# A two-layer decoder on one core: the mixer's product within sequences in two row halves, and the routed tokens in full and half tiles

## The chip, the core and the metric

The kernel runs on one core of a Trainium2 chip, in float32 throughout. The metric is the time of one execution in device microseconds. TensorE (PE) multiplies matrices, and its weight loads are shown as an engine of their own (PEld); VectorE is DVE, ScalarE is ACT, GpSimd is POOL, and SyncE (SP) issues transfers.

## What is computed

The input is 64 sequences of 64 tokens of width 256, so 4096 tokens. Two layers follow each other, each with three blocks that are added to the residual stream:

```python
x = x + mixer0(layernorm(x))        # Mamba-2 scan: 4 heads of 128, state 128, one chunk of 64 = one sequence
x = x + xattn0(layernorm(x), ctx)   # attention to ctx_512, 16 heads
x = x + moe0(layernorm(x))          # 7 routed experts, the best 2 of each token, and a shared one
x = x + wkv1(layernorm(x))
x = x + gqa1(layernorm(x), ctx)
x = x + ffn1(layernorm(x))          # 8 groups of experts, computed densely
```

The change touches the first and the third of them. In the mixer a sequence is one chunk, so what matters is the product within the chunk:

```python
L = exp(where(causal, log_diff, -inf))
CB = einsum('bcign,bcjgn->bcijg', C_c, B_c)
y_intra = einsum('bcijGH,bcijG,bcjGH,bcjGHp->bciGHp', L_rs, CB, dt_rs, x_rs)
```

The routed experts are

```python
_, ids = top_k(gate + gate_bias, 2)
u = xt @ Wup[e] + bup[e]
g = silu(u @ Wgate[e] + bgate[e]) * u
eo = g @ Wdown[e] + bdown[e]
out = sum over the two chosen experts of probs * eo, plus the shared expert
```

## The kernel before

**Order of the work.** `Net.run` (line numbers are those of the kernel before) runs three phases: `layer0` (mixer, attention, and for seven of the eight blocks of 512 tokens the front of the experts), `moe_phase` (the last front, the tables, the routed tiles, some of the shared expert), and `layer1`. Each phase is a set of generators ("streams") that are played by `Plan.play`: the planner keeps a time for each engine, prices every instruction with `Plan.cost` while the program is built, and always continues the stream that can begin first. A `yield` waits for what the stream has issued; `yield [1]` also asks for one free PSUM bank, `[2]` for two; a pair such as `("made", 3)` waits for a mark. The result is a fixed order of instructions on each engine. Every engine then works through its own list in that order, and all instructions carry the line of the helper that issues them (L60), so the profile tells them apart by the names of their tiles.

**The mixer.** `ssm_front` prepares half a block (256 tokens) and `ssm_tile` works on 128 tokens, that is two sequences; there are 32 such tiles. `ssm_tile` makes `cbm` (CB with the causal mask, on DVE), `ml` (the decays, an exponential on ACT), and then their product on POOL into `ssm_m`. `ssm_m` is one of two tiles that `w_ssm` zeroes once: 128 rows, 4 heads, 128 columns, in which sequence j fills the rows and the columns of its own 64 tokens and the rest stays zero. So two POOL instructions of 64 partitions write one tile. `xdt` (inputs times dt, transposed to tokens by rows) is the other factor. The product `py` is four matmuls, one for each head, of 128 rows by 128 columns into one PSUM bank; DVE multiplies all of it by the gate `sf_sg` into `y`, POOL adds `sf_g2`, and `po` is the output projection, which DVE adds to `x_sb`.

**The routed experts.** `moe_front` finds the two best experts of each token, and `moe_row` scatters its row (the normed token and its weight) to a slot of `moe_hs` in DRAM, where expert e owns the rows from 4096 e. `moe_tables` then counts on DVE: `n` is the number of tiles of 256 rows that each expert needs, `end` their running sum, `tab` (as integers `mt_int`) gives for each of the `MAXT` tiles its expert and its first row, and `left` the row of `moe_ys` in which each token's result will lie. MAXT is (8192 + 7 x 255) / 256 = 38, the most that seven experts can need. `moe_tile` loads for tile j the expert and row with `value_load` on SP, then by transfers the rows (`ht`), the expert's three matrices (`pack`) and a bias; it transposes the rows (`ht_ps`, `htT`), and `expert` computes u (`u_ps`, `uT`), g (`g_ps`, `gT`, with a DVE product) and d (`d_ps`). DVE adds the bias, ACT scales by the weight, and POOL issues the store to `moe_ys`. Six tiles may be loaded ahead, three be in work. The shared expert (`shared`, tiles `sh_hT`, `sh_w`) fills the time until the first routed tile begins; what is left of it goes to `layer1`, where `collect` gathers the routed results into `x_sb`.

In the routed phase TensorE's order for one tile is: transposes of the next tile, d of the tile before, g of this tile, u of the next.

Of the kernel before, what the change touches and what calls it, by code (L numbers as in the profile page):

```python
# [5 lines left out]
F32 = mybir.dt.float32  # L6
I32 = mybir.dt.int32
AF = mybir.ActivationFunctionType
# [4 lines left out]
P = 128  # L13
# [18 lines left out]
ET_PER_E = NBLK * TB // ET  # L32
MAXT = (2 * NBLK * TB + 7 * (ET - 1)) // ET
# [204 lines left out]
class Net:  # L238
# [86 lines left out]
    def w_ssm(self, side):  # L325
# [8 lines left out]

        w["m"] = []
        for i in range(2):
            t = wp.tile([P, 4, P], F32, name=f"ssm_m{i}")
            nc.gpsimd.memset(t, 0.0)
            w["m"].append(t)
# [156 lines left out]
    def ssm_tile(self, wk, w, n, t, f):  # L496
# [23 lines left out]
        m = w["m"][t]  # L520
        for r in seqs:
            gp.tensor_mul(m[r, :, r], ml[r], bc(cbm[r], 1, 4))
# [8 lines left out]
        yield self.after(("g2", n, 0), ("g2", n, 2), 1)  # L531
        py = self.mm([P, 4, P], "py")
        for q in range(4):
            te.matmul(py[:, q], xdt[:, q], m[:, q], start=True, stop=True)
        yield
        y = wk.tile([P, 4, P], F32, tag="y", bufs=2, name="y")
        v.tensor_mul(y, py, f["sg"][:, :, tok])
        self.give(py)
# [206 lines left out]

    def w_moe(self, side):
# [14 lines left out]
        w["thr"] = wp.tile([P, ET_PER_E], F32, name="moe_thr")  # L761
# [143 lines left out]
    def moe_tables(self, wk, w):  # L905
# [8 lines left out]
        gt, n, end = t("gt", [P, 7, ET_PER_E]), t("n", [P, 7]), t("end", [P, 7])  # L914
        v.tensor_tensor(gt, bc(cnt, 2, ET_PER_E), bc(w["thr"], 1, 7), ALU.is_gt)
        self.give(cnt)
        v.tensor_reduce(n, gt, AX.X, ALU.add)
        v.tensor_tensor_scan(end, w["ones"][:, 0:7], n, 0.0, ALU.mult, ALU.add)
        past, st, tab = t("past", [1, MAXT, 7]), t("st", [1, MAXT]), t("tab", [1, 2, MAXT])
        v.tensor_tensor(past, bc(end[0:1], 1, MAXT), bc(w["num"], 2, 7), ALU.is_le)  # L920
        v.tensor_reduce(tab[:, 0], past, AX.X, ALU.add)
        v.tensor_mul(past, past, bc(n[0:1], 1, MAXT))
        v.tensor_reduce(st, past, AX.X, ALU.add)
        v.tensor_sub(st, w["num"], st)
        v.tensor_scalar(st, st, float(ET), None, ALU.mult)
        v.scalar_tensor_tensor(tab[:, 1], tab[:, 0], float(SLOTS), st, ALU.mult, ALU.add)
        w["tab"] = wk.tile([1, 2, MAXT], I32, tag="mt_int", bufs=1, name="mt_int")
        v.tensor_copy(w["tab"], tab)

        off, of, left = t("off", [P, 7]), t("of", [P, NBLK * 2 * NT, 7]), t("left", [P, NBLK * 2 * NT])  # L930
        v.tensor_sub(off, end, n)
        v.scalar_tensor_tensor(off, off, float(ET), w["slot"], ALU.mult, ALU.subtract)
        v.tensor_mul(of, w["oh"].rearrange("p b k t e -> p (b k t) e"), bc(off, 1, NBLK * 2 * NT))
        v.tensor_reduce(left, of, AX.X, ALU.add)
        v.tensor_add(left, left, w["at"].rearrange("p b k t -> p (b k t)"))
        v.tensor_copy(self.left.rearrange("p b k t -> p (b k t)"), left)
# [4 lines left out]
    def moe_tile(self, wk, w, j):  # L941
        nc, te, v = self.nc, self.nc.tensor, self.nc.vector
        yield self.after(("tables", 0), ("tile", j - 6))
        e = nc.sync.value_load(w["tab"][0:1, 0, j:j + 1], min_val=0, max_val=7)
        r = nc.sync.value_load(w["tab"][0:1, 1, j:j + 1], min_val=0, max_val=ROWS - ET)
        h = wk.tile([P, 2, HW], F32, tag="ht", bufs=6, name="ht")
        rd = nc.sync.dma_start(h, w["hs"][bass.ds(r, ET)].rearrange("(i p) d -> p i d", p=P)).ins
# [7 lines left out]
        yield self.after(("made", j - 3), 1)  # L955
        ps = self.mm([P, 2, ET], "ht_ps")
        for c in range(2):
            for i in range(2):
                te.transpose(ps[:, c, i * P:(i + 1) * P], h[:, i, c * P:(c + 1) * P], self.ident)
        yield  # L960
        self.plan.mark("begun", j)
        hT = wk.tile([P, 2, ET], F32, tag="htT", bufs=3, name="htT")
        v.tensor_copy(hT, ps)
        self.give(ps)
        yield [1]
        ps = yield from self.expert(wk, m, hT, 3, False)
        y = wk.tile([P, 2, D], F32, tag="y", bufs=3, name="y")
        v.tensor_add(y, ps, bc(b, 1, 2))
        self.give(ps)
        yield  # L970
        for i in range(2):
            nc.scalar.activation(y[:, i], y[:, i], AF.Copy, scale=h[:, i, D:D + 1])
# [765 lines left out]
```

## Time and profile before

| what | us |
|---|---|
| median of 3 runs | 2133.9 |
| lowest and highest of them | 2132.7 and 2133.91 |
| the profiled execution's own time | 2130.03 |
| span of its trace, first to last instruction | 2128.3 |
| PE, DVE, ACT, POOL busy | 1943.1, 1343.9, 797.0, 871.3 |
| mean granted TensorE clock | 0.962 |

In a timeline a line gives the start and the length in us, the engine, the line of the kernel, the operation, the tiles it writes and reads, the shapes, how many records were merged (x8), and in brackets how long the engine had been idle before and what ended that. A matmul in float32 leaves two records, a transpose one. Matmuls overlap at their ends, so that the distance from the first start of a group to the first start of the next tells what the group costs. Shapes of a matmul are weights (rows*columns), then what is moved (rows x columns).

### The profile page before, as it was taken

The page shows a single profiled execution, that of the slowest core. Times are in us where ns is not written, and L with a number is a line of the kernel's source. Part 1 is how long each engine was busy: PE and PEld are TensorE (multiplying, and loading weights), DVE is VectorE, ACT ScalarE, POOL GpSimd, SP SyncE. Part 2 cuts the span into 40 slices and gives each one's busy share as a digit, 9 for nine tenths or more (in the row PEclk, how much of TensorE's full clock was granted, in tenths as well). Part 3 has the DMA queues.
Part 4 walks back from the last instruction along what each step waited for, and adds up shares of the span by engine and source line. Part 5 has one row for each costly group of instructions (what it writes and reads, how often), then busy time and mean ns, then how long its engine had stood idle before and what let it go on. Part 6 is the DMA issues. An engine that isn't in the chain of part 4 may idle for free. (4 is left out here: it accounts for less than half of the span.)

```text
span 2128.3 us, 35968 instructions
## 1 busy us (share of the span) xinstructions
PE 1943.1 (91%) x13515; PEld 1557.0 (73%) x13515; DVE 1343.9 (63%) x3080; ACT 797.0 (37%) x1445; POOL 871.3 (41%) x1079
## 2 busy tenths in 40 slices
PE   7998998989889997899997879979899999999998
PEld 6777787767667776788875647767677777777777
DVE  5668677777776764333336787887778676755331
ACT  3435343343434333344443433433334334343220
POOL 3333535345443423111126856666455344432211
PEclk9999999999989999999998879999999999999999
DMA  7965000001000011588844111121011101010010
GB/s 202 346 205 162 22 16 22 24 14 34 17 20 18 22 38 59 190 291 266 267 149 101 26 24 28 22 35 22 17 26 23 19 11 20 8 24 14 14 26 10
DMA packets 168765, 152.02 MB, mean 71 GB/s; under 512 B 76153, under 2 KB 156176, under 8 KB 168592
## 3 DMA queue, kind: packets, MB, share of 16 engines
q1 hardware_dynamic: 153232, 122.44, 19.8%
q0 software_dynamic: 15360, 27.28, 5.2%
q8 instruction: 107, 1.75, 0.3%
q14 instruction: 66, 0.54, 0.1%
HBM read 88.84 MB, written 60.83 MB: 70 GB/s over the span
## 5 line engine op out<-in xcount | busy, mean ns | idle before, releaser
L60 PE MATMUL gu_ps<-hT,ffn_gu 128*128 128x256 f32 x1408 | 337.6, 387 | 4.7 <-DVE gqa_q L60 3.9
L60 PEld LDWEIGHTS gu_ps<-hT,ffn_gu 128*128 128x128 f32 x1408 | 260.7, 192 | 50.4 <-issue 8.1
L60 PE MATMUL acc<-ffn_d,aT 128*128 128x256 f32 x704 | 165.5, 388 | 9.2 <-DVE aT L60 9.2
L60 POOL TENSOR_TENSOR aT<-aT,ffn_sc 128x512 f32<-128x512 f32 (+1 forms) x48 | 69.2, 1442 | 228.9 <-DVE aT L60 202.7
L60 PEld LDWEIGHTS acc<-ffn_d,aT 128*128 128x128 f32 x704 | 134.1, 194 | 34.2 <-DVE aT L60 10.7
L60 PE MATMUL proj<-sf_hT,w_in 128*128 128x256 f32 x640 | 152.3, 396 | 0.0
L60 ACT ACT_TABLE_LOAD x104 | 133.4, 1283 | 18.4 <-PE st L60 7.9
L60 PEld LDWEIGHTS proj<-sf_hT,w_in 128*128 128x128 f32 x640 | 124.5, 198 | 19.5 <-issue 1.6
L60 PE MATMUL po<-xa_vo,ctxT 128*128 128x256 f32 x512 | 119.0, 388 | 12.2 <-DVE ctxT L60 6.3
L60 ACT ACTIVATE aT<-gu_ps 128x512 f32<-128x512 f32 x96 | 48.7, 559 | 204.5 <-PE gu_ps L60 204.4
L60 DVE TENSOR_TENSOR aT<-aT,gu_ps 128x512 f32<-128x512 f32 x96 | 56.9, 633 | 106.2 <-ACT aT L60 106.2
L60 PE MATMUL q_ps<-xn_hT,xa_q 128*128 128x256 f32 x512 | 117.5, 385 | 4.4 <-ACT xn_hT L60 3.7
L60 PEld LDWEIGHTS po<-xa_vo,ctxT 128*128 128x128 f32 x512 | 97.5, 194 | 29.4 <-issue 11.3
L60 POOL DMA_INDIRECT x_sb<-moe_ys,left x64 | 106.3, 1661 | 20.4 <-issue 11.2
L60 POOL DMA_DIRECT2D moe_ys<-y x38 | 27.3, 717 | 212.8 <-ACT y L60 205.8
L60 PEld LDWEIGHTS q_ps<-xn_hT,xa_q 128*128 128x128 f32 x512 | 96.4, 192 | 23.5 <-ACT xn_hT L60 5.5
L60 POOL TENSOR_TENSOR ssm_m<-ml,cbm 64x256 f32<-64x256 f32 x64 | 46.4, 725 | 144.1 <-ACT ml L60 123.2
L60 DVE TENSOR_REDUCE gqa_q<-sc 128x8 f32<-128x512 f32 x128 | 79.2, 680 | 36.8 <-PE sc L60 34.1
L60 DVE SCALAR_TENSOR_TENSOR sf_acc<-proj,ssm_vec,sf_acc 128x252 f32<-128x252 f32 (+2 forms) x192 | 87.3, 472 | 11.3 <-ACT sf_acc L60 6.7
L60 POOL DMA_INDIRECT moe_hs<-moe_h,moe_slots x64 | 64.5, 1007 | 63.6 <-DVE moe_h L60 31.0
L60 DVE TENSOR_TENSOR x_sb<-x_sb,po 128x256 f32<-128x256 f32 x64 | 26.4, 413 | 98.3 <-PE po L60 98.2
L60 POOL TENSOR_TENSOR p<-p,sm 128x1024 f32<-128x1024 f32 x32 | 60.6, 1901 | 56.0 <-DVE sm L60 39.7
(338 smaller groups left out, 4381.9 us busy)
## 6 DMA issues: line engine op xcount, KB each, us to landing
moe_hs<-moe_zero SPq DMA_DIRECT2D x30, 1088.0 KB
pack<-in_moe_pack_dram SPq DMA_DIRECT2D x38, 770.0 KB
ht<-moe_hs SPq DMA_DIRECT2D x38, 272.0 KB
moe_ys<-y POOLq DMA_DIRECT2D x38, 256.0 KB
bias<-moe_bias SPq DMA_DIRECT2D x38, 128.0 KB
x_sb<-in_x_dram SPq DMA_DIRECT2D x8, 512.0 KB
moe_hT<-mr_hT SPq DMA_DIRECT2D x8, 512.0 KB
sh_hT<-moe_hT SPq DMA_DIRECT2D x16, 256.0 KB
```

The costliest lines, as they stand in the source:

```text
L60: return do(*a, **k)
```

## The change

Two parts of the kernel are changed.

**Mixer.** `ssm_m` is no longer a zeroed tile of 128 by 128 per head but a tile of 128 rows by 64 columns per head (`wk.tile([P, 4, S])`, two buffers), written by one POOL product of 128 partitions; the two tiles that were zeroed at the start are gone. `py` becomes two PSUM tiles in two banks, one for each sequence. For each head there are two matmuls, of rows 0 to 63 and of rows 64 to 127, with 128 weight columns and 64 moved columns each. DVE multiplies each of the two by its part of the gate, in two instructions. The stream asks for two free banks where it asked for one.

**Routed experts.** The tiles are now `FULL` = 8192 / 256 = 32 full tiles of 256 rows and MAXT - FULL half tiles of 128 rows. The formula gives 32 + (8192 + 7 x 127) / 128 - 64 = 38 for MAXT, so six half tiles. An expert's rows are counted in halves; its pairs of halves go to the full tiles, an odd half to a half tile, and pairs beyond the 32nd are split over the half tiles that are left. The tables take more steps for it, and `left` three selections instead of one. `left` is now made after the second routed tile (`yield [("made", 2)]`), the table of tiles as before ahead of the first. Half tiles are spread evenly between the full ones (`order`), and `expert` works on 128 columns where the tile is half. The planner's marks go by the place in that order (`at`).

```diff
-ET_PER_E = NBLK * TB // ET
-MAXT = (2 * NBLK * TB + 7 * (ET - 1)) // ET
+HET = ET // 2
+HALVES = NBLK * TB // HET
+FULL = 2 * NBLK * TB // ET
+MAXT = FULL + (2 * NBLK * TB + 7 * (HET - 1)) // HET - 2 * FULL
...
-        w["m"] = []
-        for i in range(2):
-            t = wp.tile([P, 4, P], F32, name=f"ssm_m{i}")
-            nc.gpsimd.memset(t, 0.0)
-            w["m"].append(t)
...
-        m = w["m"][t]
-        for r in seqs:
-            gp.tensor_mul(m[r, :, r], ml[r], bc(cbm[r], 1, 4))
+        m = wk.tile([P, 4, S], F32, tag="m", bufs=2, name="ssm_m")
+        gp.tensor_mul(m, ml, bc(cbm, 1, 4))
         yield self.after(("xs", n, 0), ("xs", n, 2), 1)
         pxt = self.mm([P, 4, P], "pxt")
         for q in range(4):
@@ -528,14 +523,17 @@
         xdt = wk.tile([P, 4, P], F32, tag="xdt", bufs=2, name="xdt")
         v.tensor_mul(xdt, pxt, bc(f["dt"][:, t], 2, P))
         self.give(pxt)
-        yield self.after(("g2", n, 0), ("g2", n, 2), 1)
-        py = self.mm([P, 4, P], "py")
+
+        yield self.after(("g2", n, 0), ("g2", n, 2), 2)
+        py = [self.mm([P, 4, S], "py") for _ in seqs]
         for q in range(4):
-            te.matmul(py[:, q], xdt[:, q], m[:, q], start=True, stop=True)
+            for j, r in enumerate(seqs):
+                te.matmul(py[j][:, q], xdt[r, q], m[r, q], start=True, stop=True)
         yield
         y = wk.tile([P, 4, P], F32, tag="y", bufs=2, name="y")
-        v.tensor_mul(y, py, f["sg"][:, :, tok])
-        self.give(py)
+        for j, r in enumerate(seqs):
+            v.tensor_mul(y[:, :, r], py[j], f["sg"][:, :, t * P + j * S:t * P + (j + 1) * S])
+        self.give(*py)
...
-        gt, n, end = t("gt", [P, 7, ET_PER_E]), t("n", [P, 7]), t("end", [P, 7])
-        v.tensor_tensor(gt, bc(cnt, 2, ET_PER_E), bc(w["thr"], 1, 7), ALU.is_gt)
+
+        gt, nh, n, end, od, oend = t("gt", [P, 7, HALVES]), t("nh", [P, 7]), t("n", [P, 7]), t("end", [P, 7]), t("od", [P, 7]), t("oend", [P, 7])
+        v.tensor_tensor(gt, bc(cnt, 2, HALVES), bc(w["thr"], 1, 7), ALU.is_gt)
         self.give(cnt)
-        v.tensor_reduce(n, gt, AX.X, ALU.add)
+        v.tensor_reduce(nh, gt, AX.X, ALU.add)
+        v.tensor_reduce(n, gt[:, :, 1::2], AX.X, ALU.add)
+        v.scalar_tensor_tensor(od, n, -2.0, nh, ALU.mult, ALU.add)
         v.tensor_tensor_scan(end, w["ones"][:, 0:7], n, 0.0, ALU.mult, ALU.add)
-        past, st, tab = t("past", [1, MAXT, 7]), t("st", [1, MAXT]), t("tab", [1, 2, MAXT])
-        v.tensor_tensor(past, bc(end[0:1], 1, MAXT), bc(w["num"], 2, 7), ALU.is_le)
+        v.tensor_tensor_scan(oend, w["ones"][:, 0:7], od, 0.0, ALU.mult, ALU.add)
+        yield
+
+        odd = oend[:, 6:7]
+        num, k = t("num", [1, MAXT]), t("k", [1, MAXT - FULL])
+        v.tensor_copy(num[:, 0:FULL], w["num"][:, 0:FULL])
+        v.tensor_scalar(num[:, FULL:], w["num"][:, FULL:], odd[0:1], None, ALU.subtract)
+        v.tensor_scalar(k, w["num"][:, FULL:], -2.0 * FULL, None, ALU.add)
+        past, st, tab, two = t("past", [1, MAXT, 7]), t("st", [1, MAXT]), t("tab", [1, 2, MAXT]), t("two", [1, 2, 7])
+        v.tensor_scalar(two[:, 0], end[0:1], 2.0, None, ALU.mult)
+        v.tensor_scalar(two[:, 1], n[0:1], 2.0, None, ALU.mult)
+        v.tensor_tensor(past, bc(two[:, 0], 1, MAXT), bc(num, 2, 7), ALU.is_le)
         v.tensor_reduce(tab[:, 0], past, AX.X, ALU.add)
-        v.tensor_mul(past, past, bc(n[0:1], 1, MAXT))
+        v.tensor_mul(past, past, bc(two[:, 1], 1, MAXT))
         v.tensor_reduce(st, past, AX.X, ALU.add)
-        v.tensor_sub(st, w["num"], st)
-        v.tensor_scalar(st, st, float(ET), None, ALU.mult)
+        v.tensor_sub(st, num, st)
+        v.tensor_scalar(st, st, float(HET), None, ALU.mult)
         v.scalar_tensor_tensor(tab[:, 1], tab[:, 0], float(SLOTS), st, ALU.mult, ALU.add)
+        yield
+
+        nk = MAXT - FULL
+        op, is_, ok, oe = t("op", [1, nk, 7]), t("is", [1, nk, 7]), t("ok", [1, nk]), t("oe", [1, 2, nk])
+        v.tensor_tensor(op, bc(oend[0:1], 1, nk), bc(k, 2, 7), ALU.is_le)
+        v.tensor_reduce(oe[:, 0], op, AX.X, ALU.add)
+
+        v.tensor_sub(is_, bc(oend[0:1], 1, nk), bc(k, 2, 7))
+        v.tensor_scalar(is_, is_, 1.0, None, ALU.is_equal)
+        v.tensor_mul(is_, is_, bc(od[0:1], 1, nk))
+        v.tensor_mul(is_, is_, bc(n[0:1], 1, nk))
+        v.tensor_reduce(oe[:, 1], is_, AX.X, ALU.add)
+        v.tensor_scalar(oe[:, 1], oe[:, 1], float(ET), None, ALU.mult)
+        v.scalar_tensor_tensor(oe[:, 1], oe[:, 0], float(SLOTS), oe[:, 1], ALU.mult, ALU.add)
+        v.tensor_scalar(ok, k, odd[0:1], None, ALU.is_lt)
+        v.tensor_sub(oe, oe, tab[:, :, FULL:])
+        v.tensor_mul(oe, oe, bc(ok, 1, 2))
+        v.tensor_add(tab[:, :, FULL:], tab[:, :, FULL:], oe)
         w["tab"] = wk.tile([1, 2, MAXT], I32, tag="mt_int", bufs=1, name="mt_int")
         v.tensor_copy(w["tab"], tab)
-
-        off, of, left = t("off", [P, 7]), t("of", [P, NBLK * 2 * NT, 7]), t("left", [P, NBLK * 2 * NT])
-        v.tensor_sub(off, end, n)
-        v.scalar_tensor_tensor(off, off, float(ET), w["slot"], ALU.mult, ALU.subtract)
-        v.tensor_mul(of, w["oh"].rearrange("p b k t e -> p (b k t) e"), bc(off, 1, NBLK * 2 * NT))
-        v.tensor_reduce(left, of, AX.X, ALU.add)
-        v.tensor_add(left, left, w["at"].rearrange("p b k t -> p (b k t)"))
-        v.tensor_copy(self.left.rearrange("p b k t -> p (b k t)"), left)
+        self.plan.mark("tables", 0)
+        yield [("made", 2)]
+
+
+        m = NBLK * 2 * NT
+        at, oh = w["at"].rearrange("p b k t -> p (b k t)"), w["oh"].rearrange("p b k t e -> p (b k t) e")
+        off = [t(f"off{i}", [P, 7]) for i in range(3)]
+        of, sel = t("of", [P, m, 7]), [t(f"sel{i}", [P, m]) for i in range(3)]
+        v.tensor_sub(off[0], end, n)
+        v.scalar_tensor_tensor(off[0], off[0], float(ET), w["slot"], ALU.mult, ALU.subtract)
+        v.scalar_tensor_tensor(off[1], n, float(ET), w["slot"], ALU.mult, ALU.add)
+        v.tensor_sub(off[2], oend, od)
+        v.tensor_scalar(off[2], off[2], float(HET), float(FULL * ET), ALU.mult, ALU.add)
+        v.tensor_sub(off[2], off[2], off[1])
+        for i in range(3):
+            v.tensor_mul(of, oh, bc(off[i], 1, m))
+            v.tensor_reduce(sel[i], of, AX.X, ALU.add)
+            yield
+        rest, behind = t("rest", [P, m]), t("behind", [P, 1])
+        v.tensor_tensor(rest, at, sel[1], ALU.is_ge)
+        v.tensor_add(sel[0], sel[0], at)
+        v.tensor_add(sel[2], sel[2], at)
+        v.tensor_scalar(behind, odd, float(HET), None, ALU.mult)
+        v.tensor_scalar(sel[1], sel[0], float(FULL * ET), behind, ALU.is_ge, ALU.mult)
+        v.tensor_add(sel[0], sel[0], sel[1])
+        v.tensor_sub(sel[2], sel[2], sel[0])
+        v.tensor_mul(sel[2], sel[2], rest)
+        v.tensor_add(sel[0], sel[0], sel[2])
+        v.tensor_copy(self.left.rearrange("p b k t -> p (b k t)"), sel[0])
...
-    def moe_tile(self, wk, w, j):
+    def moe_tile(self, wk, w, at, j):
         nc, te, v = self.nc, self.nc.tensor, self.nc.vector
-        yield self.after(("tables", 0), ("tile", j - 6))
+        nt = 2 if j < FULL else 1
+        row = ET * min(j, FULL) + HET * max(j - FULL, 0)
+        yield self.after(("tables", 0), ("tile", at - 6))
         e = nc.sync.value_load(w["tab"][0:1, 0, j:j + 1], min_val=0, max_val=7)
-        r = nc.sync.value_load(w["tab"][0:1, 1, j:j + 1], min_val=0, max_val=ROWS - ET)
+        r = nc.sync.value_load(w["tab"][0:1, 1, j:j + 1], min_val=0, max_val=ROWS - nt * P)
         h = wk.tile([P, 2, HW], F32, tag="ht", bufs=6, name="ht")
-        rd = nc.sync.dma_start(h, w["hs"][bass.ds(r, ET)].rearrange("(i p) d -> p i d", p=P)).ins
+        rd = nc.sync.dma_start(h[:, 0:nt], w["hs"][bass.ds(r, nt * P)].rearrange("(i p) d -> p i d", p=P)).ins
...
-        yield self.after(("made", j - 3), 1)
+        yield self.after(("made", at - 3), 1)
         ps = self.mm([P, 2, ET], "ht_ps")
         for c in range(2):
-            for i in range(2):
+            for i in range(nt):
                 te.transpose(ps[:, c, i * P:(i + 1) * P], h[:, i, c * P:(c + 1) * P], self.ident)
         yield
-        self.plan.mark("begun", j)
+        self.plan.mark("begun", at)
         hT = wk.tile([P, 2, ET], F32, tag="htT", bufs=3, name="htT")
-        v.tensor_copy(hT, ps)
+        v.tensor_copy(hT[:, :, 0:nt * P], ps[:, :, 0:nt * P])
...
+        n = int(hT.shape[2])
...
-                te.matmul(pu[:, i], mats[0][c][:, i * P:(i + 1) * P], hT[:, c], start=c == 0, stop=c == 1)
+                te.matmul(pu[:, i, 0:n], mats[0][c][:, i * P:(i + 1) * P], hT[:, c], start=c == 0, stop=c == 1)
...
-                te.matmul(pg[:, i], mats[1][c][:, i * P:(i + 1) * P], uT[:, c], start=c == 0, stop=c == 1)
+                te.matmul(pg[:, i, 0:n], mats[1][c][:, i * P:(i + 1) * P], uT[:, c, 0:n], start=c == 0, stop=c == 1)
...
-        nc.vector.tensor_mul(gT, gT, uT)
+        nc.vector.tensor_mul(gT[:, :, 0:n], gT[:, :, 0:n], uT[:, :, 0:n])
...
-        for i in range(2):
+        for i in range(n // P):
...
-            self.moe_tables(wk, w)
-            self.plan.mark("tables", 0)
-
+            yield from self.moe_tables(wk, w)
+
+
+        order = sorted(range(MAXT), key=lambda j: j if j < FULL else FULL // (MAXT - FULL) * (j - FULL) + 2.5)
         self.shared_left = list(range(NH))
         with self.tc.manual_schedule():
-            self.plan.play([(0, self.moe_front(wk, w, NBLK - 1)), (0, tables())] + [(0, self.moe_tile(wk, w, j)) for j in range(MAXT)],
+            self.plan.play([(0, self.moe_front(wk, w, NBLK - 1)), (0, tables())] + [(0, self.moe_tile(wk, w, at, j)) for at, j in enumerate(order)],
```

## The prediction

> **What bounds the kernel now.** I read the stretches first (busy time of each engine, us), then the timelines of the two places that the change touches, then who waits for whom.
>
> ```profile
> 50.00:850.00 800.00, 722.87 (x4717) 581.91 (x4716) 557.74 (x1558) 309.58 (x554) 329.28 (x465) 0.95 0.22 69
> 886.00:1096.00 210.00, 209.87 (x1042) 184.14 (x1043) 75.99 (x110) 95.63 (x222) 25.83 (x36) 1.00 0.81 267
> ```
>
> The columns are PE, PEld, DVE, ACT, POOL, granted clock, DMA share, GB/s. Between 50 and 850 us (mixer and attention of the first layer) TensorE works 90% of the time; 77 us are its waits on others. Between 886 and 1096 us (the routed tiles) it never stops and its clock is full: there a saved TensorE microsecond is a saved microsecond, as long as nothing else becomes late. One period of the routed tiles, and the operations that close it:
>
> ```profile
> 963.61 1.89 PE L60 MATMUL u_ps<-htT,pack 128*128 128x256 f32 x8
> 965.34 0.60 PE L60 MATMUL ht_ps<-ident,ht 128*128 128x128 f32 x4
> 965.78 1.89 PE L60 MATMUL d_ps<-pack,gT 128*128 128x256 f32 x8
> 967.51 1.89 PE L60 MATMUL g_ps<-uT,pack 128*128 128x256 f32 x8
> 969.23 1.89 PE L60 MATMUL u_ps<-htT,pack 128*128 128x256 f32 x8
> 969.49 0.84 ACT L60 ACTIVATE gT<-g_ps,pack 128x256 f32<-128x256 f32 x2
> 970.37 0.69 DVE L60 TENSOR_TENSOR gT<-gT,uT 128x512 f32<-128x512 f32 x1 [1.97 <-ACT gT L60]
> ```
>
> Take starts, not durations: u costs 1.73, ht 0.44, d 1.73, g 1.72; a tile takes 5.62 us. A matmul in f32 is two records (two passes), so four matmuls are x8. And the way into that phase:
>
> ```profile
> 873.99 0.28 DVE L60 TENSOR_TENSOR mt_gt<-cnt,moe_thr 128x112 f32<-128x112 f32 x1 [1.16 <-PE cnt L60]
> 876.63 0.19 DVE L60 TENSOR_TENSOR mt_st<-moe_num,mt_st 1x38 f32<-1x38 f32 x1
> 877.28 0.19 DVE L60 CAST mt_int<-mt_tab 1x76 int32<-1x76 f32 x1
> 878.44 0.62 DVE L60 TENSOR_REDUCE mt_left<-mt_of 128x64 f32<-128x448 f32 x1
> 879.46 0.69 DVE L60 TENSOR_TENSOR gT<-gT,sh_hT 128x512 f32<-128x512 f32 x1
> ```
>
> ```profile
> 880.36 0.46 SPq L60 DMA_DIRECT2D pack<-in_moe_pack_dram  x1
> ```
>
> ```profile
> 886.01 1.97 PE L60 MATMUL u_ps<-htT,pack 128*128 128x256 f32 x8 [1.24 <-DMA pack<-in_moe_pack_dram]
> ```
>
> The integer table is done at 877.47, SP issues the first weights at 880.36, and TensorE, out of shared-expert work, already waits 1.24 us for them. This chain is on the path.
>
> **Half tiles (gain).** 38 full tiles become 32 full and, by the built order of TensorE, six half ones (ht_ps with two transposes occurs six times). The rest of the second layer's order on TensorE stays as it was. In a half tile u and g are four matmuls each of 128 moved columns with 128x128 weights. That shape exists: the mixer's py, 39.94 to 40.83 below, 0.89 us for eight passes. So u + g = 1.78, d with two matmuls 0.87, two transposes 0.22: 2.87 us against 5.62, saving 2.75. But the order is g of the tile before, u of the half tile, ht of the next, then d of the tile before, which needs gT: ACT and DVE finish gT at 971.06, 1.83 after g's end at 969.23. Today u and ht cover 1.73 + 0.44 = 2.17 of it; behind a half tile only 0.89 + 0.44 = 1.33. d waits 0.50. Saving 2.25 x 6 = 13.5 us. Ends: 16.5 without that wait; 9 if each half tile meets a second wait of 0.5 (uT of the next tile, ACT is shared) and u and g run at 120 ns a pass. DMA: a full tile moves 770 + 272 + 128 + 256 = 1426 KB; a half one saves 264. The mean tile falls to 5.26 us and 1384 KB, so the DMA share goes from 0.81 to about 0.84, and a pack is issued about four tiles ahead (964.44 for a use at 986.09). I cost it at nothing; without that cover a late pack would be a wait like the 1.24 above.
>
> **The tables (loss).** DVE's order shows 32 instructions from mt_gt to mt_int where there were 11 in 3.48 us. Of the 21 new ones nearly all have 6 to 42 elements in a row, like mt_st (0.19 and 0.04 to the next): 21 x 0.21 = 4.4, and 0.3 for twice as wide a threshold row and its reductions: 4.7 us. Nothing covers it: the SP loads wait for the table, u_ps for the pack, and the filling shared-expert matmuls are the same. The six instructions behind the table (877.40 to 879.5) move behind the second routed tile, so the shared gT at 879.46 is late by only 2.6, but that work ends before the pack in any case. The moved part is now 22 instructions with three wide pairs (0.62 each), in DVE's order ahead of the first half tile's gT: six small ones and a pair, 2.4 us, where d has about 1.7 to spare: 0.7 once. The idle stretch of some 5 us could cost granted clock; here, 870 to 884 with its short gaps kept 1.00. Loss 5.4; ends 4 and 8.
>
> **py in two row halves.** Per mixer tile (32 of them) four matmuls of 128 rows and 128 columns become eight of 64 rows and 64 columns. What do narrow ones cost?
>
> ```profile
> 30.32 1.57 PE L60 MATMUL xp_py<-xp_p 64*96 64x64 f32 x16
> 31.82 1.99 PE L60 MATMUL proj<-sf_hT,w_in 128*128 128x256 f32 x8
> 39.94 1.06 PE L60 MATMUL py<-ssm_m,xdt 128*128 128x128 f32 x8
> 40.83 1.90 PE L60 MATMUL xp_pw<-xp_ctxT,xp_qT 128*128 128x64 f32 x16
> 42.66 1.08 PE L60 MATMUL xp_pv<-xp_qT,xp_ctxT 128*64 128x256 f32 x8
> ```
>
> ```profile
> 1619.31 1.15 PE L60 MATMUL gu_ps<-fr_smT,ffn_mgu 32*128 32x256 f32 x16
> 1620.39 0.63 PE L60 MATMUL weT_ps<-ident,fr_sc 128*64 128x128 f32 x4
> 1624.40 1.10 PE L60 MATMUL pf<-ffn_at,fr_weT 64*128 64x64 f32 x8
> 1625.44 1.99 PE L60 MATMUL pv<-wk_mix,wkv_v 128*128 128x256 f32 x8
> ```
>
> 64 moved columns with 128-column weights: xp_pw 1.83/16 = 114 ns a pass; py with 128 moved columns 111. With 96 weight columns and 64 rows 94. pf, exactly the new shape but all in one row half, 130, some 0.15 of its 1.04 being the change of array shape. So the weights' columns set the pace, and halving rows and moved columns does not shorten a pass. What can help is overlap of the two row halves: in gu_ps of 32 rows, four groups, 16 passes take 1.08, 67 each, so loads into different row groups do overlap. For two groups, 16 x 111 / 2 + 0.15 = 1.04 us against 0.89 to 0.99 (0.94) now: +0.1 x 32 = +3.2 us. Ends: bound by moved columns alone (half of 0.89, plus 0.15: 0.59) -11.2; no overlap (16 x 130 = 2.08) +36.5.
>
> [...]
>
> **The rest of the mixer.** POOL's two products of 64x256 (0.725 each) become one of 128x256 (ul, the same shape: 0.63 to kva's 0.73): -0.72 per tile. POOL idles 123 us ahead of ssm_m for ACT's ml, so m is seldom the cause; but TensorE waits 28.1 us for POOL between 50 and 850 (y 8.6, p 7.5, the scatters 12.0) in 16 waits, at most 0.72 each: 0 to -11.5; I take -2, since the queue ahead of most is scatters and p. DVE's y from py is two instructions of 128x256 (0.41 each, as x_sb with po) for one of 0.68: +0.14 per tile, 0 to +4.5; I take +1. py now wants two PSUM banks, and layer 0 is planned anew by a planner that prices py at half: the order of py, po and pt shifts in many rounds. No row prices it; I bound it by +-6 us, less than a tenth of the 77 us of waits, and take 0.
>
> **Sum.** -13.5 + 5.4 + 3.2 - 2 + 1 = -5.9. Against the profiled execution's 2130.0 us (span 2128.3 and 1.7 around it) 2124.1; the median 2133.9 stands 3.9 above that run, so 2128.0.
>
> **Rivals.** (1) The halves run at the pace of moved columns: py -11.2 in place of +3.2, sum -20.3, 2113.6. Against it: xp_pw and pf. (2) The other side: the weight loads of two row halves do not overlap. The gu_ps row of 64 rows (12 passes in 1.50, 125 each) fits loads one after another as well as pairs. Then py is 2.08, +36.5, of which the planner, believing py short, hides nothing: sum +27.4, 2161.3. It decides from py at 0.94 + 9.1/32 = 1.22 us. For it: only four groups show overlap. (3) The gain is eaten: half tiles save 9, the table costs 8, the rest +2.2: +1.2, 2135.1. For it: gT's slack is only 0.34 us and TensorE's order is fixed. (4) That the halves are fewer or more than said is excluded by the order.
>
> **Chances.** The forecast 0.48 (own range 2121 to 2134), rival 1 0.14, rival 2 0.14, rival 3 0.24. Within 0.2% (4.3 us) counts as no change, about what a measurement of this kernel can tell. Faster: 0.36 + 0.14 + 0.02 = 0.52; same: 0.12 + 0.15 = 0.27; slower: 0.14 + 0.07 = 0.21. The range runs from rival 1, 2113, to 2145, where py would take 1.6 us; left out is the far part of rival 2.
>
> **What would show it.** In the changed profile: py x16 from start to next start near 1.05 (0.6: rival 1; 2: rival 2); u and g of 128 columns at 0.9; a wait of d_ps on gT of 0.5 at each half tile; mt_gt to mt_int near 8.2; first u_ps waiting for the pack about 4 us; mixer stretch within 6 us of before. I am wrong if the routed tiles end less than 4 us earlier relative to cnt than before, or if the mixer's stretch moves by more than 10 us.

## The result, and the profile after

| | us |
|---|---|
| before, median of 18 runs | 2133.9 |
| after, median of 17 runs | 2123.5 |
| ratio, with its 95% interval | 0.9954 (0.9945 to 0.9963) |
| the profiled execution before: time, span | 2130.03, 2128.3 |
| the profiled execution after: time, span | 2121.44, 2119.7 |

One more execution of the changed kernel took 2862.9 us at a granted clock of 0.64 and is not counted; with it the median is the 2123.8 that the expectations below name. By the ratio the change takes 9.8 us off (7.9 to 11.7, the interval times 2133.9); 5.9 were forecast. To find where the time went I take from TensorE's records of each profile the start of `cnt`, of the first routed `u_ps` and of the last pass of the last routed `d_ps` (its group begins 1.62 us earlier), and the end of the span:

| us | before | after | difference | forecast |
|---|---|---|---|---|
| start to `cnt` (mixer, attention) | 873.67 | 875.20 | +1.5 | +2.2 |
| `cnt` to first `u_ps` (tables) | 12.34 | 14.55 | +2.2 | +4.7 |
| first `u_ps` to last `d_ps` (routed tiles) | 215.78 | 205.64 | -10.1 | -12.8 |
| last `d_ps` to the end (second layer) | 1026.48 | 1024.28 | -2.2 | 0 |

The stretches of the profile after, in the columns of the prediction (PE, PEld, DVE, ACT, POOL, granted clock, DMA share, GB/s):

```profile
50.00:850.00 800.00, 726.97 (x4955) 585.26 (x4955) 554.10 (x1587) 309.81 (x554) 306.86 (x435) 0.95 0.21 69
886.00:1096.00 210.00, 203.31 (x1034) 176.99 (x1033) 79.29 (x137) 91.47 (x220) 25.58 (x37) 0.99 0.80 267
```

In the first, POOL has 22.4 us less to do and TensorE 4.1 more; nothing got shorter. In the second TensorE now has waits, most of them ahead of its first `u_ps`, which starts only at 889.75, and the DMA share did not rise (0.80, 0.81 before). The product of the mixer, TensorE's timeline after:

```profile
39.17 1.11 PE L62 MATMUL py<-ssm_m,xdt 64*128 64x64 f32 x16
40.21 2.00 PE L62 MATMUL xp_pw<-xp_ctxT,xp_qT 128*128 128x64 f32 x16
```

From start to start 1.04 us, 65 ns a pass, as worked out; it is 1.04 in all 18 places where one such group can be told from its neighbours. In the single records of this group, which the timeline merges, two passes start 6 or 7 ns apart and the next two 112 ns behind them (160 behind the first two). So a pair of passes, one from each row half, takes what one pass of 128 rows took before (111 to 112 ns). A half tile among full ones, same view:

```profile
937.23 1.89 PE L62 MATMUL g_ps<-uT,pack 128*128 128x256 f32 x8
938.96 1.05 PE L62 MATMUL u_ps<-htT,pack 128*128 128x128 f32 x8
939.85 0.60 PE L62 MATMUL ht_ps<-ident,ht 128*128 128x128 f32 x4
940.90 1.99 PE L62 MATMUL d_ps<-pack,gT 128*128 128x256 f32 x8 [0.45 <-DVE gT L62]
942.73 1.05 PE L62 MATMUL g_ps<-uT,pack 128*128 128x128 f32 x8
943.62 1.89 PE L62 MATMUL u_ps<-htT,pack 128*128 128x256 f32 x8
```

u and g take 0.89 us each (938.96 to 939.85, 942.73 to 943.62) where a full tile takes 1.73, and the d of the tile before waits for gT, because only 0.89 + 0.44 lie between g's end and it. The 0.45 in brackets count from the recorded end of `ht_ps`; from start to start `ht_ps` takes 1.05 instead of 0.44, and the d behind it 1.83 instead of 1.73, so that this wait costs 0.71. The way into the routed tiles, DVE first, then SP, then TensorE:

```profile
875.52 0.39 DVE L62 TENSOR_TENSOR mt_gt<-cnt,moe_thr 128x224 f32<-128x224 f32 x1 [1.16 <-PE cnt L62]
...
877.08 0.15 DVE L62 TENSOR_SCALAR mt_k<-moe_num 1x6 f32<-1x6 f32 x1
877.15 0.15 DVE L62 TENSOR_SCALAR mt_two<-mt_end 1x7 f32<-1x7 f32 x1
...
880.25 0.17 DVE L62 TENSOR_SCALAR mt_is<-mt_is 1x42 f32<-1x42 f32 x1
880.46 0.19 DVE L62 TENSOR_TENSOR mt_is<-mt_is,mt_od 1x42 f32<-1x42 f32 x1
...
881.91 0.16 DVE L62 TENSOR_TENSOR mt_tab<-mt_tab,mt_oe 1x12 f32<-1x12 f32 x1
882.11 0.19 DVE L62 CAST mt_int<-mt_tab 1x76 int32<-1x76 f32 x1
882.22 0.67 DVE L62 TENSOR_TENSOR gT<-gT,sh_hT 128x512 f32<-128x512 f32 x1
```

```profile
885.15 0.37 SPq L62 DMA_DIRECT2D pack<-in_moe_pack_dram  x1
```

```profile
883.04 3.69 PE L62 MATMUL d_ps<-sh_w,gT 128*128 128x256 f32 x16 [0.84 <-DVE gT L62]
887.39 0.63 PE L62 MATMUL ht_ps<-ident,ht 128*128 128x128 f32 x4 [0.66 <-DMA ht<-moe_hs]
889.75 3.60 PE L62 MATMUL u_ps<-htT,pack 128*128 128x256 f32 x8 [1.73 <-DMA pack<-in_moe_pack_dram]
893.14 0.69 PE L62 MATMUL ht_ps<-ident,ht 128*128 128x128 f32 x4
```

The chain from `mt_gt` to the end of `mt_int` grew from 3.48 to 6.78 us, and the issue of the first pack moved by as much, from 6.69 to 9.95 us behind the start of `cnt`. From that issue to the first `u_ps` it then took 4.60 us, against 5.65 before. The first `u_ps` then takes 3.39 us (889.75 to 893.14) where the same eight passes took 1.80 before, at a granted clock of 1.00: between 889.7 and 893.2 us it is 0.53.

### The profile page after: what moved, and what is told of

It is laid out like the page before. It is cut to its first block, busy times and chain, and to the rows that moved or that the text cites. A ratio compares the mean times of both kernels' runs of the same rounds, so it can differ in the third digit from the quotient of the medians.

```text
span 2119.7 us, 36371 instructions
## 1 busy us (share of the span) xinstructions
PE 1933.7 (91%) x13735; PEld 1548.6 (73%) x13735; DVE 1343.7 (63%) x3149; ACT 791.1 (37%) x1439; POOL 845.6 (40%) x1045
## 5 line engine op out<-in xcount | busy, mean ns | idle before, releaser
L62 DVE SCALAR_TENSOR_TENSOR sf_acc<-proj,ssm_vec,sf_acc 128x252 f32<-128x252 f32 (+2 forms) x192 | 87.3, 472 | 7.5 <-ACT sf_acc L62 3.0
L62 ACT COPY qT<-pq 128x512 f32<-128x512 f32 x64 | 37.4, 586 | 115.2 <-PE pq L62 115.2
```

What stands on the lines that cost most here:

```text
L62: return do(*a, **k)
```

## The experiments

Twelve more programs were run, one of them the changed kernel itself. The table has the marks of their profiles, in us. The second layer's instructions stand in one and the same order on TensorE, DVE, ACT and POOL in all of them but one (`halves_last`), and TensorE's order up to `cnt` is that of the kernel before in the first two rows, that of the changed kernel in all others but the last.

| kernel | start to `cnt` | to first `u_ps` | to last `d_ps` | to the end | median of runs | ratio to before |
|---|---|---|---|---|---|---|
| before | 873.67 | 12.34 | 215.78 | 1026.48 | 2133.9 | |
| experts_only | 875.76 | 16.18 | 206.35 | 1022.40 | 2122.5 | 0.9949 (0.9935 to 0.9962) |
| mixer_only | 875.96 | 12.03 | 215.90 | 1026.82 | 2132.7 | 0.9998 (0.9988 to 1.0007) |
| after | 875.20 | 14.55 | 205.64 | 1024.28 | 2123.5 | 0.9954 (0.9945 to 0.9963) |
| after_again | 881.92 | 16.54 | 206.14 | 1021.83 | 2125.3 | 0.9953 (0.9935 to 0.9970) |
| py_grouped | 883.25 | 14.68 | 205.66 | 1027.43 | 2129.9 | 0.9982 (0.9972 to 0.9992) |
| m_twice | 872.79 | 14.45 | 205.51 | 1024.39 | 2119.7 | 0.9941 (0.9928 to 0.9955) |
| halves_padded | 876.17 | 15.17 | 218.66 | 1020.80 | 2133.4 | 1.0004 (0.9993 to 1.0015) |
| tables_long | 876.76 | 19.33 | 204.00 | 1020.77 | 2123.5 | 0.9956 (0.9942 to 0.9971) |
| warm_first | 876.77 | 16.05 | 204.01 | 1024.32 | 2119.3 | 0.9933 (0.9916 to 0.9949) |
| warm_short | 875.32 | 16.38 | 204.22 | 1027.01 | 2123.8 | 0.9958 (0.9945 to 0.9972) |
| halves_last | 876.43 | 16.34 | 206.01 | 1040.14 | 2134.5 | 1.0007 (0.9994 to 1.0020) |
| halves_late | 874.57 | 14.70 | 206.32 | 1026.91 | 2125.0 | 0.9964 (0.9953 to 0.9974) |
| warm_m_twice | 881.96 | 16.19 | 204.01 | 1028.22 | 2130.4 | 0.9978 (0.9962 to 0.9994) |

**Each part alone.** `mixer_only` is the kernel before with the diff's lines in `w_ssm` and `ssm_tile` and nothing else; `experts_only` is the changed kernel with those lines taken back.

> The kernel before with the mixer's part alone (tables and 38 full tiles as before). Theory, the gain is the half tiles' and the mixer is worth nothing: py costs 1.04 us instead of 0.94 to 0.99 (+2 us over 32 tiles), POOL's fused product and the new order give as much back; the time within 3 us of before, cnt within 3 us of 873.7. Rival, the mixer has a good part of the measured 10 us, through POOL's 23 us or the new order: 4 to 7 us faster than before.

> The changed kernel with the mixer of before, so layer 0 runs in the order of before. Theory: cnt at 873.7 as before, first routed u 2 to 4 us later than before, last routed d 6 to 9 us earlier; the time 7 to 10 us under before and within 3 us of the changed kernel. Rival (the mixer shares the gain): 3 to 6 us under before.

The mixer's part is worth -0.4 us (-2.6 to +1.5), the experts' part -10.9 (-13.9 to -8.1). The gain is the experts', all of it; within their intervals the two parts add up to what both bring. In its profile `experts_only` has `cnt` at 875.76, 2.1 us behind the kernel before although TensorE's order up to there is the same, so the +1.5 of the table above is not shown to be the mixer's; partly for that reason its last routed `d_ps` came 3.5 us earlier and not 6 to 9.

**The order of py's passes.** The same sixteen passes, but all of one row half and then all of the other:

```diff
-        for q in range(4):
-            for j, r in enumerate(seqs):
+        for j, r in enumerate(seqs):
+            for q in range(4):
                 te.matmul(py[j][:, q], xdt[r, q], m[r, q], start=True, stop=True)
```

> The changed kernel with py's matmuls issued half by half: four heads of rows 0 to 63, then four of rows 64 to 127, instead of alternating; all else in the same order. Theory, two row halves overlap only when neighbours in the order belong to different halves: py x16 from 1.04 to about 1.9 us (16 x 111 ns + 0.15), the mixer's stretch and the time +20 to +27 us against the changed kernel. Rival, TensorE finds the other half's loads over eight passes: py stays at 1.04 us and the time does not change.

TensorE's timeline of this kernel:

```profile
39.68 1.60 PE L62 MATMUL py<-ssm_m,xdt 64*128 64x64 f32 x16
41.21 2.00 PE L62 MATMUL xp_pw<-xp_ctxT,xp_qT 128*128 128x64 f32 x16
```

1.53 us from start to start instead of 1.04, 96 ns a pass instead of 65, in all 18 single groups. In the single records the passes of one half start 112 ns apart here too, but the second half's eight begin with the fifth pass of the first half: four passes of the first half and four of the second go alone. So passes of different row halves run side by side, and the order decides how many do; that none would in this order (about 1.9 us) was wrong, since the second half starts ahead of three passes that were issued before it. Over the 32 groups py takes 13.0 us more. `cnt` comes 8.1 us later than in the profile after, the offset growing mostly in steps of 0.5 us, what one py lost, with some of it won back at waits; the median is 6.4 us higher, not 20 to 27. Half to 60% of a slower py is felt.

**POOL's product in two instructions.** The new `ssm_m`, written by two products of 64 partitions; the planner is shown only the first, so that the order stays as it is:

```diff
-        gp.tensor_mul(m, ml, bc(cbm, 1, 4))
+        r0, r1 = seqs
+        gp.tensor_mul(m[r0], ml[r0], bc(cbm[r0], 1, 4))
+        gp.real.tensor_mul(m[r1], ml[r1], bc(cbm[r1], 1, 4))
```

> The changed kernel with the product into ssm_m again in two POOL instructions of 64 partitions each (every engine's order kept): POOL +0.72 us in each of 32 tiles, 23 us in all. Theory, m is seldom late: 0 to +3 us against the changed kernel, POOL's busy time up by 23 us. Rival, POOL's queue is what the mixer waits for: +6 to +12 us.

POOL is busy for 328.9 us between 50 and 850 us again, as before, and the kernel is not slower. TensorE's waits for POOL in that stretch come to 24.2 us, 25.6 in the profile after. So the 22 us that POOL saves are not shown to be worth anything.

**What the half tile saves.** The same tables, loads and stores of half a tile, but the work of a full tile on TensorE, ScalarE and VectorE (except for the last step, `y`):

```diff
-            for i in range(nt):
-                te.transpose(ps[:, c, i * P:(i + 1) * P], h[:, i, c * P:(c + 1) * P], self.ident)
+            for i in range(2):
+                te.transpose(ps[:, c, i * P:(i + 1) * P], h[:, i % nt, c * P:(c + 1) * P], self.ident)
...
-        v.tensor_copy(hT[:, :, 0:nt * P], ps[:, :, 0:nt * P])
+        v.tensor_copy(hT, ps)
...
-        ps = yield from self.expert(wk, m, hT[:, :, 0:nt * P], 3, False)
+        ps = yield from self.expert(wk, m, hT, 3, False)
```

> The changed kernel, but TensorE, ScalarE's uT and gT and VectorE's htT and gT do a full tile's work for each of the six half tiles (both 128-column halves hold the same rows); loads, y and stores stay those of half a tile. Theory: the gain is TensorE's, 16 more passes of 128x256 worth 111 ns each and the second transposes, 2.75 us a half tile less the wait of 0.4 that goes: the stretch from the first routed u_ps to the last d_ps grows from 205.6 by 12 to 15 us and the time to 2136 to 2139, above the kernel before by the price of the tables. Rival: in this stretch the DMA engines are busy 80% of the time and the smaller loads and stores are what pays: the stretch grows by 5 us at most, the time to at most 2129.

The routed stretch grows by 13.0 us, 2.17 for each half tile, and the time by 9.9: the gain was the engines' work, with TensorE the one that never stopped before (busy 209.87 of 210 us), and not the transfers. The time of 2133.4 lies below the 2136 to 2139 expected, so the price of the tables does not show in it; in this profile the second layer is 3.5 us shorter than in the changed kernel's. What TensorE waited for between 889 and 1100 us (total, times, longest), in the changed kernel and then in this one:

```profile
PE d_ps L62 <- DVE gT L62: 4.0, 7, 1.7
PE u_ps L62 <- DMA pack<-in_moe_pack_dram: 1.7, 1, 1.7
```

```profile
PE u_ps L62 <- DMA pack<-in_moe_pack_dram: 2.4, 1, 2.4
PE g_ps L62 <- ACT uT L62: 0.8, 2, 0.6
```

The waits of d for gT go with the half tiles. One of the seven is the last tile's 1.72, which the kernel before had too (in `halves_padded` it lies behind 1100 us); the other six make 2.3 us by the brackets, 0.38 each, and 3.9 us from start to start, 0.65 each.

**Longer tables.** Sixteen more small instructions ahead of the conversion:

```diff
+        for _ in range(16):
+            v.tensor_scalar(tab, tab, 0.0, None, ALU.add)
         w["tab"] = wk.tile([1, 2, MAXT], I32, tag="mt_int", bufs=1, name="mt_int")
```

> The changed kernel with 16 more small VectorE operations on the 1x2x38 table, one after the other, ahead of its conversion to integers; values unchanged. Theory: the chain from cnt to mt_int lies bare in front of the routed tiles, TensorE waits for it with nothing to do; at 0.08 to 0.21 us from one start to the next that is 1.3 to 3.4 us, the first routed u_ps comes as much later behind cnt (14.55 us in the changed kernel's profile), and the time is 2125 to 2127. Rival: the chain is covered by the two shared d_ps and by the load of the first pack; u_ps comes less than 0.7 us later and the time stays within 1 us of 2123.8.

DVE's and TensorE's timelines of this kernel:

```profile
883.67 3.52 DVE L62 TENSOR_SCALAR mt_tab<-mt_tab 1x76 f32<-1x76 f32 x16
887.23 0.19 DVE L62 CAST mt_int<-mt_tab 1x76 int32<-1x76 f32 x1
887.35 1.27 DVE L62 TENSOR_TENSOR gT<-gT,sh_hT 128x512 f32<-128x512 f32 x2
```

```profile
888.17 5.24 PE L62 MATMUL d_ps<-sh_w,gT 128*128 128x256 f32 x16 [4.40 <-DVE gT L62]
893.25 0.60 PE L62 MATMUL ht_ps<-ident,ht 128*128 128x128 f32 x4
896.09 1.97 PE L62 MATMUL u_ps<-htT,pack 128*128 128x256 f32 x8 [2.24 <-DMA pack<-in_moe_pack_dram]
```

The sixteen take 3.56 us, 0.22 each, where each reads what the one ahead of it wrote. The shared expert's gT stands behind them in DVE's list, so d_ps waits 4.40 instead of 0.84: not one of the sixteen is hidden. The first `u_ps` comes 4.78 us later behind `cnt`, more than the 1.3 to 3.4 expected: 3.56 are the sixteen, and the other 1.22 lie between the issue of the first pack and `u_ps` (5.82 us against 4.60). Now d_ps is the slow one (5.08 us, 888.17 to 893.25, against 3.65 before) and `u_ps` runs at its full pace (1.80 us, 896.09 to 897.89). Up to the last routed `d_ps` 3.1 us are lost. Yet the time did not rise: in this profile the second layer, in the same order, took 3.5 us less, and the median of the runs equals the changed kernel's. The chain lies bare where it stands; that its length reaches the end was not shown.

**The clock of the first routed tile.** Idle 128x128 matmuls, two passes each, fill TensorE's gaps: once 5 and 14 of them, once 2 and 7 (shown; `warm` is 0 for all but the first tile):

```diff
+        for _ in range(0 if at else 2):
+            te.real.matmul(ps[:, 0, 0:P], self.ident, self.ident, start=True, stop=True)
         for c in range(2):
             for i in range(nt):
                 te.transpose(ps[:, c, i * P:(i + 1) * P], h[:, i, c * P:(c + 1) * P], self.ident)
...
         pu = self.mm([P, 2, ET], "u_ps")
+        for _ in range(warm):
+            te.real.matmul(pu[:, 0, 0:P], self.ident, self.ident, start=True, stop=True)
...
-        ps = yield from self.expert(wk, m, hT[:, :, 0:nt * P], 3, False)
+        ps = yield from self.expert(wk, m, hT[:, :, 0:nt * P], 3, False, warm=0 if at else 7)
```

> The changed kernel with 19 idle 128x128 passes on TensorE in the gaps ahead of the first routed tile: five before its ht_ps, 14 between that and its u_ps, overwritten by it. Theory: the eight passes of the first u_ps took 3.4 us instead of 1.73 from start to the next because the granted clock fell to 0.53 after TensorE had waited 3.2 of 7 us; with the gaps filled they take 1.73 to 1.9, the start of u_ps behind cnt stays near 14.5 us, and what follows comes 1.4 to 1.7 us earlier: about 2122. Rival: the clock falls at that place for another reason, a budget over a longer time: the eight passes take 3 us or more all the same, or the next ones do, and the time stays within 1 us of 2123.8.

> As the kernel with 19 idle passes, but two and seven: a pass of 128x128 in f32 stood twice in the trace, so that 19 of them filled 4.4 us and put the first u_ps 1.5 us later, which gave back what its full clock had gained. Theory: two and seven fill about 0.45 and 1.55 us of the gaps; the first u_ps starts 14.3 to 14.8 us behind cnt (14.55 in the changed kernel), its eight passes take 1.73 to 2.0 us from start to the next, and the last routed d_ps comes 1.2 to 1.7 us nearer to cnt than the changed kernel's 220.2; the time falls by as much, to 2122. Rival: so short a filling does not hold the clock: the eight passes take 2.5 us or more and the time stays at 2123.8.

TensorE's timeline with the short filling:

```profile
887.95 1.73 PE L1043 MATMUL u_ps<-ident 128*128 128x128 f32 x14
891.70 1.97 PE L62 MATMUL u_ps<-htT,pack 128*128 128x256 f32 x8 [2.03 <-DMA pack<-in_moe_pack_dram]
894.05 0.66 PE L62 MATMUL ht_ps<-ident,ht 128*128 128x128 f32 x4 [0.39 <-DMA ht<-moe_hs]
```

With both fillings the first `u_ps` runs at its full pace (1.89 us long with the long one and 1.97 with the short, 3.60 in the changed kernel), and the routed stretch is 204.0 and 204.2 us instead of 205.6. So 1.5 us of the changed kernel's routed stretch are the clock of 0.53. But the first pack landed late in this profile, 6.43 us from its issue to `u_ps` against 4.60, and `u_ps` started 16.38 us behind `cnt` instead of 14.3 to 14.8; nothing is left up to the last `d_ps`, and the median did not move. The long filling had the lowest median of all (2119.3), but its profile shows no gain up to the last `d_ps` either and its interval overlaps that of the changed kernel; I don't call it faster.

**Where the half tiles stand.** First all of them behind the full ones, then in a row ahead of the last full tile:

```diff
-        order = sorted(range(MAXT), key=lambda j: j if j < FULL else FULL // (MAXT - FULL) * (j - FULL) + 2.5)
+        order = list(range(MAXT))
```

```diff
+        order = list(range(FULL - 1)) + list(range(FULL, MAXT)) + [FULL - 1]
```

> The changed kernel with its six half tiles played behind the 32 full ones instead of one after every five; the same work. Theory: what is saved belongs to each half tile, wherever it stands, less a wait of about 0.4 us of its d_ps on gT: the stretch from the first routed u_ps to the last routed d_ps is 205.6 us in the changed kernel's profile and stays within 1.5 us of it, and the time within 2 us of 2123.8. Rival: the spacing carries the gain, since the work of a full neighbour is what covers a half tile's shorter chain (u_ps, uT, g_ps, gT, d_ps); with six in a row each stalls TensorE about 1 us more, the stretch grows to 211 to 212 and the time to about 2130.

> The changed kernel with the six half tiles in a row behind 31 full tiles, and the last full tile behind them. With the half tiles at the very end the routed stretch kept its length (206.0 us against 205.6), but the planner then ordered layer 1 otherwise on every engine, and the stretch behind the last routed d_ps took 1040 us instead of 1024. Here layer 1's instructions stand in the changed kernel's order. Theory: that other order of layer 1 is what cost 10.7 us, not half tiles in a row: the time comes back to within 3 us of 2123.8 and the stretch behind the last d_ps to 1021 to 1027 us. Rival: half tiles in a row cost, by their transfers and stores, which fall together and are felt later: the time stays at 2130 to 2135 although the order of layer 1 is restored.

At the end they cost 11.0 us by the medians, though the routed stretch is 206.0 us long. TensorE's waits behind 1100 us, in `halves_last` and then in `halves_late`:

```profile
PE wk_hT L62 <- ACT wk_h L62: 16.3, 3, 6.8
PE d_ps L62 <- DVE gT L62: 6.8, 3, 3.0
PE st L62 <- DVE gqa_q L62: 6.1, 2, 3.5
```

```profile
PE pq L62 <- POOL gqa_q L62: 11.7, 6, 4.0
PE wk_hT L62 <- ACT wk_h L62: 9.6, 1, 9.6
PE acc L62 <- DVE aT L62: 9.2, 5, 4.1
```

In the first the second layer is in another order, with other waits; in the second, one full tile moved behind the half ones is enough for the planner to give the old order back, and the time comes back to 2125.0. The rival fell: six half tiles in a row cost about 1.5 us by the medians, within the intervals of the two, and the rest of the 11 came with the planner's new order of the layer behind them. (The profiled run of `halves_last`, 2140.7, lies 6 us above its median, so its 1040 us are more than the typical excess.) The waits are other ones, but they are not longer in sum. The stretch behind the last routed `d_ps`, in the same two kernels:

```profile
1098.00:2138.00 1040.00, 952.63 (x7389) 739.55 (x7389) 669.16 (x1294) 368.31 (x620) 488.70 (x527) 0.95 0.14 27
1095.00:2122.00 1027.00, 939.67 (x7390) 734.36 (x7388) 669.99 (x1294) 362.93 (x617) 490.50 (x527) 0.96 0.14 26
```

TensorE is idle for 87.4 and 87.3 us in them; all 13 us lie in its busy time, for the same work at a lower granted clock (0.95 against 0.96). So in these profiles the new order costs by the clock that it was granted. Why the clock is lower in it was not tried, and the clock need not be all: the six executions of `halves_last` with a mean clock of 0.955 to 0.959 took 2127.8 to 2133.8 us, and those of `halves_late`, at 0.955 to 0.960, took 2121.3 to 2134.1.

**Two small gains together, and the changed kernel once more.** `warm_m_twice` has the short filling and both POOL products, here both shown to the planner.

> The short filling and ssm_m's product in two GpSimd instructions, in one kernel. The product in two gave 2119.7 and the long filling 2119.3, each about 4 us under the changed kernel, though the marks of their profiles explain 2.6 and 0. Theory: these 4 us are mostly scatter between programs of nearly the same work: together they give 2119 to 2123, no sum. Rival: both are gains of their own and add: 2114 to 2117.

> The changed kernel itself, beside the three others on the same chip, as the mark that they are compared with. Theory: 2122.5 to 2125, and the 4 us between it and the two faster variants are theirs. Rival: on this chip it is itself at 2119 to 2121, and they gained nothing.

Neither the theory nor the rival of the first foresaw 2130.4. Here the planner saw the second POOL instruction, and layer 0 came out in another order (TensorE's list up to `cnt` differs in 39 places); `cnt` comes at 881.96, the granted clock being 1.00 between 67 and 80 us, where the last section finds 0.51. So this kernel says nothing on whether gains add; by its profile (`cnt` 6.8 us later) and by the medians (6.9) such a re-plan of layer 0 can cost some 7 us. The changed kernel came out at 2125.3 in six runs from 2115.4 to 2128.2, just above what was expected of it. A median of five or six runs is good to some 2 us at best, so the 4 us of `m_twice` and `warm_first` are not shown to be gains.

## Why the prediction was right, and where not

The direction and the place were right: the routed tiles gain, the mixer does not. The forecast of 2128.0 was 4.5 us above the median. Step by step:

- **py: right, and its share of the time too dear.** 1.04 us was worked out from two row halves that run in pairs, each pair at the pace of one full pass, and 1.04 was measured; two groups in a row take 1.93, so the 0.15 of a group (0.05 ahead of its second pair, 0.10 behind its last) is paid once. Rival 1 (0.59) and rival 2 (2.08) both fall, and `py_grouped` shows what the 1.04 hangs on: the alternating order. But +3.2 over 32 tiles was too much. The groups before took 0.89 to 1.09 from start to start, mostly more than the 0.94 assumed, and after the change two tiles that follow each other pay it once; summed over all groups py takes 31.3 us before and 32.3 after, with one group before that holds a wait and one after at a granted clock of 0.50 priced like the others (an estimate): +1.0. Passes of one row half start 112 ns apart with half the rows and half the moved columns, as the passes of all rows did (111 to 112), so the shorter pass of rival 1 was not there. Sixteen of them took 1.04 us against the 1.9 to 2.08 estimated above for one after another, nearly twice the pace; but the zeroed tile already did both sequences in one pass of 128 rows, so twice the passes at twice the pace gain nothing over it.
- **The mixer as a whole: a little too dear.** +2.2 was forecast, `mixer_only` gives -0.4 (-2.6 to +1.5). Of py's +3.2 only +1.0 was there, and of a slower py only half to 60% is felt. POOL's -2 was not there either (`m_twice`), so the two errors cancel. DVE's +1 was not tried by itself.
- **Half tiles: right, 4 to 13% less than forecast.** 2.25 us each was forecast. `halves_padded` gives 2.17; the stretch of 204.0 us in the kernels whose first `u_ps` has its full pace gives (215.78 - 204.0) / 6 = 1.96. The passes that go are worth 2.75, as worked out. The wait of d for gT is the term that was too small: 0.50 was taken, and from start to start it costs 0.59 to 0.70 at each half tile, 0.65 on the mean. Two smaller stalls of 0.45 and 0.22 us near half tiles bring what is lost to 0.76 each, which leaves 1.99. No late pack came after the first.
- **Tables: the term that was mis-sized.** +4.7 was forecast, for 21 more small instructions at 0.21 each and 0.3 for the wider row. The chain grew by 3.3, to 6.8 us where 8.2 was named as the sign, and the first `u_ps` waited 1.73 us for the pack and not about 4. The step that failed is taking one spacing for all of them: in the new chain instructions that don't need the one ahead start 0.07 to 0.12 us apart (`mt_two` after `mt_k`, 877.08 to 877.15), and only those that do are 0.2 apart (`mt_is`, 880.25 to 880.46), as `tables_long` has it with 0.22 for each of sixteen. The 0.7 us more for the moved part did not appear: the d of the first half tile waits 0.33, less than the others. The first `u_ps` came 2.2 us later in one profile of the changed kernel and 4.2 in the other: the pack is issued 9.95 us behind `cnt` in both, and from there to `u_ps` it takes 4.60 us in the one and 6.59 in the other.
- **The granted clock: named, and taken at nothing.** At 0.53 it cost 1.6 us at the first `u_ps`. The chain's 3.3 and the clock's 1.6 make 4.9 for the 5.4 forecast, and -11.8 stands against -13.5: the errors cancel in part. That up to the last routed `d_ps` the forecast of -8.1 meets -7.9 is luck besides, since the first pack came 1.0 us sooner behind its issue than before; in the second profile of the same kernel it is -5.4.
- **What is left.** The forecast had nothing behind the routed tiles; the profiles differ by -2.2 there. With the old experts that stretch took 1026.5 and 1026.8 us, with the new ones, in the same order of instructions, 1020.8 to 1028.2 in eleven profiles, 1024.4 on the mean. Whether 2 us of the gain lie there or the medians and the profiles merely differ by so much stays open.
- **Rival 3** (half tiles save 9, tables cost 8) is out: 11.8 and, with the clock, 4.9.

## What to carry to other kernels

Where TensorE never waits, a tile cut in half is worth the passes that go, less what the following engines then lack in cover (here 0.8 of 2.75 us), and a chain of small VectorE instructions in front of it cost 0.1 us here for each that is independent and 0.2 for each that is not. Let small matmuls that share the array by row halves alternate between the halves: here the same sixteen passes took 1.04 us alternating and 1.53 grouped. Alternating, a pair cost as much here as one pass over all rows (112 ns), so that splitting a zero-filled product into halves saved nothing. In a kernel whose order is planned from prices, compare the order of the stages that were not touched before explaining a time: moving one tile gave 9.5 us (`halves_last` to `halves_late`), none of it where the tile was. And measure a wait from start to start: what the brackets show left out more than a third of it.

## What was not expected of the hardware

The same kernel, profiled twice, differed by 6.7 us in the start of `cnt`, and nearly all of it came in some 12 us. TensorE's timeline after, then in `after_again`:

```profile
67.82 2.00 PE L62 MATMUL xp_pw<-xp_ctxT,xp_qT 128*128 128x64 f32 x16
69.75 1.08 PE L62 MATMUL xp_pv<-xp_qT,xp_ctxT 128*64 128x256 f32 x8
```

```profile
68.86 3.67 PE L62 MATMUL xp_pw<-xp_ctxT,xp_qT 128*128 128x64 f32 x16
72.46 1.98 PE L62 MATMUL xp_pv<-xp_qT,xp_ctxT 128*64 128x256 f32 x8
```

The stretches around it in `after_again`:

```profile
60.00:67.00 7.00, 7.00 (x55) 6.29 (x53) 5.16 (x14) 2.38 (x6) 0.00 (x0) 1.00 1.11 353
67.00:80.00 13.00, 13.00 (x59) 9.35 (x59) 3.71 (x12) 1.94 (x3) 2.81 (x4) 0.51 1.12 350
```

Between 67 and 80 us the granted clock was 0.51 (1.00 in the profile after), with TensorE busy for all of the 7 us ahead of it. That is not the case of the first `u_ps`, ahead of which TensorE had worked 0.63 of 3 us, and which ran at its full pace when the gaps were filled (1.89 and 1.97 us long, 3.60 in the changed kernel). What halved the clock here was not shown. It means that one profile of this kernel can be off by 7 us in a stage that nothing changed, and that a mark is to be compared over several profiles.
